# Cross-attention block: query columns put into row order at their eviction from PSUM, the residual rows loaded by one DMA, and four steps of blocks 1 to 3 moved

## The chip, the core and the metric

The kernel runs on one core of a Trainium2 chip. The core has five engines with a queue of instructions each, worked off in order: TensorE (PE, matrix products into PSUM; its weight loads are listed as PEld), VectorE (DVE), ScalarE (ACT), GpSimd (POOL) and SyncE (SP), which here issues every DMA. Engines wait for one another by semaphores. The metric is the device time of one execution in microseconds, the median of several runs. Before the change it is 1155.88 us (three runs, 1151.93 to 1157.17). Profiles come from one further execution each.

## What is computed

For 16 batches of 1024 rows of 512 numbers, with 64 context rows and one condition vector a batch, all float32:

```python
xq  = ada_ln(x_q,  t_vec, Wss_q)      # layer norm, scale and shift from t_vec
xkv = ada_ln(x_kv, t_vec, Wss_kv)
q = (xq @ Wq + bq)                    # 16 heads of 32
k, v = split(xkv @ Wkv + bkv)
attn = softmax(q @ k.T / sqrt(32))    # over the 64 context rows
out = attn @ v
return x_q + (out @ Wp + bp)          # residual rows added at the end
```

## The kernel before

**Blocks.** The rows are worked in 32 blocks of 512 rows (`NB` = 32 by batches of 16 times `BPB` = 2; the code's assertions fix `B` = 16), so block `i` is one half of batch `i // 2`. A block's x tile is `[128 partitions, t = 4, 512]`: partition p and index t hold row 128 t + p.

**Steps of a block**, each a function that issues its instructions on fixed engines:

- `load_x(i)` (L104): one 1 MB DMA. `q_stats`, `q_scale` (L248, L254): row statistics on DVE (L234, L235), a square root on ACT (L240), a reciprocal on DVE (L241) and two small operations on POOL (L242, L243). `hidden` (L269): four normalisations in place on ACT (L265).
- `turn` and `move` (L394 to L416): four 32x32 block transposes on DVE (L399) into `ht`, then 16 DMAs of 64 KB (L412) that give `xt`, features on partitions. The row 128 t + 32 g + b of the block now stands in column (g, t, b). Only block 0 is turned by TensorE instead (`first_features`) and keeps its columns in the order of rows.
- `queries(i, o)` for o = 0 to 3 (L435): eight matrix instructions `pq` (L445), then one ACT eviction with bias into `qt` (L452). The columns of `qt` stay in the order (g, t, b).
- `scores(i, z)` for the two halves z of the keys (L456): 32 small matmuls `ps` (L463) into two PSUM tiles of the pool `ps_s`, which has two buffers; for each a maximum on DVE (`m`, L474) and then a copy to SBUF on ACT (L481). The next user of `ps_s` waits for these copies.
- `maxima` (L500) combines the halves and spreads them (`mb`, L495, DVE); `subtract` (L506) takes them off the two score tiles, by default on POOL; `weights` (L512) is the exponential on ACT; `sums`, `inverse` (L516, L529) are on DVE; `divide` (L536) is on POOL by default.
- `mix(i)` (L543): 64 small matmuls `po` (L559), into `ps_s` or, with `apart=False`, into four banks of the pool `ps_m`, which has four buffers; `mixed` copies them to `ot` on ACT (L579).
- `project(i, g)` (L583): eight matrix instructions `pp` (L586) on 128 columns of `ot`, into a bank of `ps_m`; `projected` (L597) adds the residual on DVE into `ob` (L599; three buffers) and issues the 256 KB write of the result (L600). With `later=True` the caller places `projected` itself.
- `load_residual(i)` (L118): four DMAs of 256 KB (L123) bring the same rows of x again, in the order that `project` gives; `residual` adds the projection's bias to them on POOL (L276).

Since the columns of `ot` stand in the order (g, t, b), `project(i, g)` yields the rows 128 t + 32 g + b for one g: four runs of 32 rows. `by_group` (L110) is the view that both the residual load and the result's write use. For block 0 the view is 128 consecutive rows:

```python
if i == 0:
    return rows[g * P : (g + 1) * P, :]
return rows.rearrange("(t g p) h -> g t p h", t=NT, g=4)[g]
```

**What sets the order.** The program is scheduled by hand (`manual_schedule`): each engine runs its instructions in the order in which the calls stand in the text. L605 to L727 write blocks 0 to 2 out call by call, L730 to L784 are a loop over the blocks 3 to 29 (`NB - 2` = 30), and L788 to L834 write out the last two blocks, y = 30 and z = 31. In the loop the residual rows of block i are asked for after the first queries of block i + 1; near the end `load_residual(NB - 1)` stands behind `move` (L758) and `load_residual(y)` behind `project(y - 2, 3)` (L792). The tile of the residual rows of block i takes the place of that of block i - 2, so its load waits for `projected(i - 2, 3)`.

Of the kernel before, what the change touches and what calls it, by code (L numbers as in the profile page):

```python
# [9 lines left out]
F32 = mybir.dt.float32  # L10
AF = mybir.ActivationFunctionType
# [4 lines left out]
P = 128  # L16
# [4 lines left out]
def cross_attention_block(  # L21
# [36 lines left out]
    nc = tc.nc  # L58

    B, LQ, H = x.shape  # L60
# [5 lines left out]
    TB = 512  # L66
    NT = TB // P
    BPB = LQ // TB
# [7 lines left out]
    xpool = ctx.enter_context(tc.tile_pool(name="xpool", bufs=2))  # L76
# [5 lines left out]
    obpool = ctx.enter_context(tc.tile_pool(name="obpool", bufs=3))  # L82
# [7 lines left out]
    def bank(name):  # L90
        return ps_m.tile([P, TB], F32, tag="mm", name=name)
# [5 lines left out]
    ctx_tiles, x_tiles, r_tiles = {}, {}, {}  # L97

    def load_context(b):
        t = kvpool.tile([P, H], F32, tag="ctx", name=f"ctx_{b}")  # L100
        nc.sync.dma_start(t, context[b : b + 2].rearrange("b k h -> (b k) h"))
        ctx_tiles[b] = t

    def load_x(i):  # L104
        b, s = divmod(i, BPB)
        t = xpool.tile([P, NT, H], F32, tag="x", name=f"x_{i}")
        nc.sync.dma_start(t, x[b, s * TB : (s + 1) * TB, :].rearrange("(t p) h -> p t h", p=P))
        x_tiles[i] = t

    def by_group(a, i, g):  # L110

        b, s = divmod(i, BPB)
        rows = a[b, s * TB : (s + 1) * TB, :]
        if i == 0:
            return rows[g * P : (g + 1) * P, :]
        return rows.rearrange("(t g p) h -> g t p h", t=NT, g=4)[g]

    def load_residual(i):  # L118

        tag = "r" if i < NB - 1 else "x"  # L120
        r = xpool.tile([P, 4, H], F32, tag=tag, name=f"r_{i}")
        for g in range(4):
            nc.sync.dma_start(r[:, g, :], by_group(x, i, g))  # L123
        r_tiles[i] = r

    w_ss = {}
# [30 lines left out]
    b_p_sb = const.tile([P, H], F32, name="b_p_sb")  # L157
# [74 lines left out]
    def row_stats(mv, r):  # L232
        bs = small.tile([P, 6], F32, tag="bs", name="bs")
        nc.vector.bn_stats(bs, r)  # L234
        nc.vector.bn_aggr(mv, bs)  # L235
# [12 lines left out]
    def q_stats(i, ts=range(NT)):  # L248
        if ts[0] == 0:
            q_mv[i] = small.tile([P, NT, 2], F32, tag="mvq", name=f"mvq_{i}")  # L250
        for t in ts:
            row_stats(q_mv[i][:, t, :], x_tiles[i][:, t, :])

    def q_scale(i):  # L254
        q_rstd[i] = rstd_of(q_mv.pop(i), NT, "q")

    def kv_stats(b):
        kv_mv[b] = small.tile([P, 1, 2], F32, tag="mvk", name=f"mvk_{b}")
        row_stats(kv_mv[b][:, 0, :], ctx_tiles[b])
# [9 lines left out]
    def hidden(i, ts):  # L269

        for t in ts:
            normalise(x_tiles[i][:, t, :], x_tiles[i][:, t, :], q_rstd[i], t)

    def residual(i):
        for g in range(4):
            nc.gpsimd.tensor_add(r_tiles[i][:, g, :], r_tiles[i][:, g, :], b_p_sb)  # L276


    k_tiles, v_tiles, xk_tiles, hk_tiles = {}, {}, {}, {}
# [77 lines left out]
    xt_tiles, qt_tiles, wq_tiles, ht_tiles = {}, {}, {}, {}  # L357


    bqs = const.tile([P, NC, BW], F32, name="bqs")  # L360
# [45 lines left out]
    def move(i):  # L406

        ht = ht_tiles.pop(i)
        xt = qpool.tile([P, 4, NC, NT * 32], F32, tag="xt", name=f"xt_{i}")
        for k in range(4):  # L410
            for g in range(4):
                nc.sync.dma_start(  # L412
                    xt[32 * k : 32 * k + 32, g],
                    ht[32 * g : 32 * g + 32, k].rearrange("p c t b -> p c (t b)"),
                )
        xt_tiles[i] = xt  # L416
# [18 lines left out]
    def queries(i, o, spare=False):  # L435

        xt, b = xt_tiles[i], i // BPB
        if o == 0:
            qt_tiles[i] = qpool.tile([P, NC, TB], F32, tag="qt", name=f"qt_{i}")
        if spare:  # L440
            pq = ps_s.tile([P, 2, TB], F32, tag="s", name=f"pq_{i}_{o}")[:, 0, :]
        else:
            pq = bank(f"pq_{i}_{o}")
        for c in range(NC):
            nc.tensor.matmul(  # L445
                pq.rearrange("p (g n) -> p g n", g=4),
                lhsT=wq_tiles[b][:, c, o * P : (o + 1) * P],
                rhs=xt[:, :, c, :],
                start=(c == 0),
                stop=(c == NC - 1),  # L450
            )
        nc.scalar.activation(qt_tiles[i][:, o, :], pq, AF.Identity, bias=bqs[:, o, b : b + 1])  # L452

    s_tiles, m_tiles = {}, {}

    def scores(i, z):  # L456

        kt, qt = k_tiles[i // BPB], qt_tiles[i]
        pss = [ps_s.tile([P, 2, TB], F32, tag="s", name=f"ps_{i}_{z}_{e}") for e in range(2)]
        for r in range(HPC):  # L460
            rows = slice(32 * r, 32 * r + 32)
            for c in range(NC):
                nc.tensor.matmul(  # L463
                    pss[r // 2][32 * c : 32 * c + 32, r % 2, :],
                    lhsT=kt[rows, c, z * HK : (z + 1) * HK],
                    rhs=qt[rows, c, :],
                    start=True,
                    stop=True,
                )
        if z == 0:  # L470
            m_tiles[i] = small.tile([P, 2, HPC, NJ], F32, tag="m2", name=f"m2_{i}")
        s_sb = big.tile([P, HPC, TB], F32, tag="big", name=f"s_{i}_{z}")
        for e in range(2):
            nc.vector.tensor_reduce(  # L474
                m_tiles[i][:, z, 2 * e : 2 * e + 2, :],
                pss[e].rearrange("p r (j a) -> p r j a", a=32),
                AX.X,
                ALU.max,
                apply_transpose=True,
            )  # L480
            nc.scalar.copy(s_sb[:, 2 * e : 2 * e + 2, :], pss[e])  # L481
        s_tiles[i, z] = s_sb

    def both(dst, src, op):

        nc.vector.tensor_reduce(dst, src.rearrange("p z r j -> p (r j) z"), AX.X, op)
# [13 lines left out]
    def maxima(i):  # L500

        m = small.tile([P, HPC * NJ], F32, tag="m", name=f"m_{i}")
        both(m, m_tiles.pop(i), ALU.max)
        mb_tiles[i] = spread(i, m, f"mb_{i}")

    def subtract(i, eng=nc.gpsimd, zs=(0, 1)):  # L506
        for z in zs:
            eng.tensor_tensor(s_tiles[i, z], s_tiles[i, z], mb_tiles[i], ALU.subtract)  # L508
# [7 lines left out]
    def sums(i, z):  # L516
        if z == 0:
            l_tiles[i] = small.tile([P, 2, HPC, NJ], F32, tag="l2", name=f"l2_{i}")
        nc.vector.tensor_reduce(  # L519
            l_tiles[i][:, z],  # L520
            s_tiles[i, z].rearrange("p r (j a) -> p r j a", a=32),
            AX.X,
            ALU.add,
            apply_transpose=True,
        )
# [3 lines left out]
    def inverse(i):  # L529

        v = small.tile([P, HPC * NJ], F32, tag="v", name=f"v_{i}")
        both(v, l_tiles.pop(i), ALU.add)
        nc.vector.reciprocal(v, v)
        vb_tiles[i] = spread(i, v, f"vb_{i}")

    def divide(i, eng=nc.gpsimd):  # L536
        vb = vb_tiles.pop(i)
        for z in range(2):
            eng.tensor_tensor(s_tiles[i, z], s_tiles[i, z], vb, ALU.mult)  # L539

    po_tiles, ot_tiles = {}, {}
# [38 lines left out]

    pp_tiles = {}

    def project(i, g, later=False):  # L583
        pp = bank(f"pp_{i}_{g}")
        for c in range(NC):
            nc.tensor.matmul(  # L586
                pp,
                lhsT=ot_tiles[i][:, c, g * P : (g + 1) * P],
                rhs=w_p_sb[:, c, :],
                start=(c == 0),  # L590
                stop=(c == NC - 1),
            )
        pp_tiles[i, g] = pp
        if not later:
            projected(i, g)

    def projected(i, g):  # L597
        ob = obpool.tile([P, H], F32, tag="ob", name=f"ob_{i}_{g}")
        nc.vector.tensor_add(ob, pp_tiles.pop((i, g)), r_tiles[i][:, g, :])  # L599
        nc.sync.dma_start(by_group(out, i, g), ob)  # L600
        if g == 3:
            r_tiles.pop(i)


# [59 lines left out]
    divide(0)  # L664
    queries(2, 0)
    scores(1, 0)
    q_stats(3, (0, 1))
    queries(2, 1)
    scores(1, 1)
    maxima(1)  # L670
    queries(2, 2)
    q_stats(3, (2, 3))
    q_scale(3)
    subtract(1)
    mix(0, apart=False)
    mixed(0)
    queries(2, 3, spare=True)
    hidden(3, range(NT))
    turn(3, range(NT))
    move(3)  # L680
    project(0, 0)
    q_stats(4)
    kv_stats(2)
    weights(1, 0)
    sums(1, 0)
    weights(1, 1)
    project(0, 1)
    q_scale(4)
    kv_scale(2)
    context_hidden(2)  # L690
    residual(1)
    sums(1, 1)
    project(0, 2)


    load_x(5)
    scores(2, 0)
    inverse(1)
    project(0, 3)
    scores(2, 1)  # L700
    divide(1, nc.vector)
    maxima(2)
    subtract(2)
    load_residual(2)
    queries(3, 0)
    hidden(4, range(NT))
# [81 lines left out]
    y, z = NB - 2, NB - 1  # L788
# [41 lines left out]
    mix(z)  # L830
    mixed(z)
    project(y, 3)
    for g in range(4):
        project(z, g)  # L834

# [1 line left out]
_INS = [  # L837
# [37 lines left out]
```

## Time and profile before

| | |
|---|---|
| median of three runs | 1155.88 us (1151.93 to 1157.17) |
| profiled execution, its own time | 1154.13 us |
| span of the profiled instructions | 1152.3 us |
| mean granted TensorE clock | 0.994 |
| DVE busy | 789.0 us (68%) |
| ACT busy | 643.5 us (56%) |
| POOL busy | 708.3 us (61%) |
| DMA moved | 145.28 MB, mean 126 GB/s |
| L445 `pq` / L586 `pp` on PE | 467.2 / 462.7 us, 1024 matrix instructions each |
| L452 eviction of the queries on ACT | 128 of 686 ns |
| L276 residual add on POOL | 128 of 1278 ns, 84.8 us of waiting for the loads of r before them |

The page gives busy time and its share of the span for each engine; groups of instructions by source line, with their number, the busy time, the mean of one and the idle time of the engine before them with what ended it; and a chain of work, followed back from the last instruction to whatever released each step. Other views are the waits (who waited for whom), the timeline (instructions in order of time, merged, with the idle time before each in brackets) and tables of busy time by stretch. "DMA share" is the busy share of the core's 16 DMA engines. All times count from the start of the span.

### The profile page before, as it was taken

Reading aid. Unit: us, or ns where it says so; the run is one execution under the profiler, and the core shown is the slowest. Engines: PE = TensorE matmul, PEld = TensorE weight load, DVE = VectorE, ACT = ScalarE, POOL = GpSimd, SP = SyncE. Lnnn points to the kernel's source line nnn. Section 1 sums busy time; section 2 is a strip of 40 time slices with the busy share of each in tenths; the row PEclk is TensorE's granted clock in tenths of the full one; section 3 lists DMA queues with packets and bytes.
Section 4 is the critical chain, followed back from the end, with each engine's and each line's share of the span. In section 5 each row is a group of like instructions: output and inputs, shape, how many; then the busy total and the mean of one; then the engine's idle time right before and its main releaser. Section 6 shows DMA issues by size and latency. Waiting matters only on the chain.

```text
span 1152.3 us, 18883 instructions
## 1 busy us (share of the span) xinstructions
PE 1121.2 (97%) x7578; PEld 488.8 (42%) x7578; DVE 789.0 (68%) x968; ACT 643.5 (56%) x752; POOL 708.3 (61%) x332
## 2 busy tenths in 40 slices
PE   6999999999999999999999999999999999999797
PEld 3533354344544445444443445343454444544242
DVE  4679657766577775767757676766657776566592
ACT  4665736656265673657546565665636667265330
POOL 0064775776576674787656678477666677487330
PEclk9999999999999999999999999999999999999899
DMA  9534334343433343443433443333433333333212
GB/s 355 173 126 145 104 99 135 131 131 121 124 113 126 134 134 112 131 127 107 137 121 125 131 132 105 128 131 123 131 102 128 137 134 124 113 104 99 98 29 82
DMA packets 79944, 145.28 MB, mean 126 GB/s; under 512 B 9928, under 2 KB 10080, under 8 KB 79856
## 3 DMA queue, kind: packets, MB, share of 16 engines
q1 hardware_dynamic: 79856, 144.07, 38.9%
q8 instruction: 60, 0.98, 0.3%
q14 instruction: 28, 0.23, 0.1%
HBM read 77.97 MB, written 33.55 MB: 97 GB/s over the span
## 4 chain that ended last, share of the span: by engine, by line
PE 91%; DVE 4%; DMA 2%; ACT 1%; POOL 1%; issue 1%; SPq 0%; DVEq 0%; POOLq 0%
PE pq L445 37%; PE pp L586 36%; PE po L559 6%; PE ps L463 6%; PE pv L338 3%; PE pk L310 2%; DMA out_dram<-ob 1%; DVE l L519 1%; POOL s L539 1%; DMA wss_q<-in_L_xcond_Wss_q_dram 1%; DVE m L474 1%; DVE ob L599 0%; DVE mb L495 0%; DVE s L508 0%; DVE bs L234 0%
## 5 line engine op out<-in xcount | busy, mean ns | idle before, releaser
L445 PE MATMUL pq<-xt,wq 128*128 128x512 f32 x1024 | 467.2, 600 | 0.0
L586 PE MATMUL pp<-w_p_sb,ot 128*128 128x512 f32 x1024 | 462.7, 596 | 0.0
L508 POOL TENSOR_TENSOR s<-s,mb 128x2048 f32<-128x2048 f32 x58 | 262.3, 4548 | 224.6 <-DVE mb L495 224.6
L445 PEld LDWEIGHTS pq<-xt,wq 128*128 128x128 f32 x1024 | 188.8, 190 | 261.6 <-issue 259.9
L586 PEld LDWEIGHTS pp<-w_p_sb,ot 128*128 128x128 f32 x1024 | 191.2, 190 | 254.4 <-issue 244.7
L539 POOL TENSOR_TENSOR s<-s,vb 128x2048 f32<-128x2048 f32 x60 | 270.2, 4528 | 36.7 <-DVE vb L495 30.5
L481 ACT COPY s<-ps 128x1024 f32<-128x1024 f32 x128 | 129.4, 1012 | 240.2 <-DVE m L474 232.8
L276 POOL TENSOR_TENSOR r<-r,b_p_sb 128x512 f32<-128x512 f32 x128 | 161.3, 1278 | 84.9 <-DMA r<-in_x_dram 84.8
L599 DVE TENSOR_TENSOR ob<-pp,r 128x512 f32<-128x512 f32 x128 | 85.8, 672 | 163.4 <-PE pp L586 128.4
L452 ACT ACTIVATE qt<-pq,bqs 128x512 f32<-128x512 f32 x128 | 87.8, 686 | 161.2 <-PE pq L445 158.0
L519 DVE TRANSPOSE_TENSOR_REDUCE l<-s 128x64 f32<-128x2048 f32 x64 | 147.4, 2305 | 32.3 <-ACT s L514 32.1
L474 DVE TRANSPOSE_TENSOR_REDUCE m<-ps 128x32 f32<-128x1024 f32 x128 | 152.3, 1228 | 23.9 <-PE ps L463 23.7
L514 ACT ACTIVATE s<-s 128x2048 f32<-128x2048 f32 x64 | 122.2, 1911 | 30.7 <-POOL s L508 26.0
L234 DVE BATCH_NORM_STATS2 bs<-x 128x6 f32<-128x512 f32 x128 | 85.5, 668 | 41.0 <-DMA x<-in_x_dram 40.9
L265 ACT ACTIVATE x<-x,rstdq 128x512 f32<-128x512 f32 x128 | 96.6, 809 | 5.8 <-POOL rstdq L243 5.8
L399 DVE STREAM_TRANSPOSE ht<-x 128x512 f32<-128x512 f32 x124 | 78.1, 683 | 10.6 <-ACT x L265 7.2
L559 PE MATMUL po<-s,vt 32*32 32x512 f32 x2048 | 78.1, 612 | 7.4 <-ACT s L481 7.4
L463 PE MATMUL ps<-qt,kt 32*32 32x512 f32 x2048 | 75.9, 600 | 3.3 <-ACT s L481 2.4
L495 DVE STREAM_TRANSPOSE mb<-m 128x2048 f32<-128x2048 f32 x32 | 74.0, 2312 | 6.4 <-POOL s L539 3.1
L495 DVE STREAM_TRANSPOSE vb<-v 128x2048 f32<-128x2048 f32 x32 | 74.0, 2311 | 3.2
L579 ACT COPY ot<-po 128x1024 f32<-128x1024 f32 (+1 forms) x66 | 61.9, 990 | 18.8 <-PE po L559 16.0
L559 PEld LDWEIGHTS po<-s,vt 32*32 32x32 f32 x2048 | 26.6, 104 | 53.7 <-issue 48.0
(73 smaller groups left out, 447.5 us busy)
## 6 DMA issues: line engine op xcount, KB each, us to landing
x<-in_x_dram SPq DMA_DIRECT2D x32, 1024.0 KB
r<-in_x_dram SPq DMA_DIRECT2D x128, 256.0 KB
out_dram<-ob SPq DMA_DIRECT2D x128, 256.0 KB
xt<-ht SPq DMA_DIRECT2D x496, 64.0 KB
wss_q<-in_L_xcond_Wss_q_dram SPq DMA_DIRECT2D x2, 1024.0 KB
ctx<-in_ctx_dram SPq DMA_DIRECT2D x8, 256.0 KB
wss_kv<-in_L_xcond_Wss_kv_dram SPq DMA_DIRECT2D x2, 1024.0 KB
w_kv_sb<-in_L_xcond_Wkv_dram SPq DMA_DIRECT2D x1, 2048.0 KB
```

Source lines behind the costliest of these rows:

```text
L276: nc.gpsimd.tensor_add(r_tiles[i][:, g, :], r_tiles[i][:, g, :], b_p_sb)
L445: nc.tensor.matmul(pq.rearrange("p (g n) -> p g n", g=4), lhsT=wq_tiles[b][:, c, o * P : (o + 1) * P], rhs=xt[:, :, c, :], start=(c == 0), ...
L463: nc.tensor.matmul(pss[r // 2][32 * c : 32 * c + 32, r % 2, :], lhsT=kt[rows, c, z * HK : (z + 1) * HK], rhs=qt[rows, c, :], start=True, s ...
L474: nc.vector.tensor_reduce(m_tiles[i][:, z, 2 * e : 2 * e + 2, :], pss[e].rearrange("p r (j a) -> p r j a", a=32), AX.X, ALU.max, apply_tra ...
L481: nc.scalar.copy(s_sb[:, 2 * e : 2 * e + 2, :], pss[e])
L495: nc.vector.transpose(t, src.unsqueeze(2).to_broadcast([P, HPC * NJ, 32]))
L508: eng.tensor_tensor(s_tiles[i, z], s_tiles[i, z], mb_tiles[i], ALU.subtract)
L514: nc.scalar.activation(p, p, AF.Exp, scale=SCALE)
L519: nc.vector.tensor_reduce(l_tiles[i][:, z], s_tiles[i, z].rearrange("p r (j a) -> p r j a", a=32), AX.X, ALU.add, apply_transpose=True,)
L539: eng.tensor_tensor(s_tiles[i, z], s_tiles[i, z], vb, ALU.mult)
L559: nc.tensor.matmul(po[c][32 * r : 32 * r + 32, :], lhsT=vt[rows, z, 32 * r : 32 * r + 32], rhs=p[rows, r, :], start=(z == 0), stop=(z == 1),)
L586: nc.tensor.matmul(pp, lhsT=ot_tiles[i][:, c, g * P : (g + 1) * P], rhs=w_p_sb[:, c, :], start=(c == 0), stop=(c == NC - 1),)
```

## The change

Three things are altered.

1. `queries` writes `qt` in the order of rows for all blocks but 0: source and destination of the ACT eviction are viewed with the axes g, t, b, and the destination's are (t, g, b) in memory. All that follows (scores, maxima, `ot`) then has its columns in the order of rows.
2. `by_group` goes. A new `rows_of` gives the view "row 128 t + p at partition p, index t" that `load_x` had. The residual rows come by one DMA of 1 MB instead of four of 256 KB, and a project's result, now 128 consecutive rows, is written to one index t of the same view.
3. In the calls written out for blocks 1 to 3, the statistics of block 3 are taken in one piece and their scale sooner; the subtraction of block 1 is asked for right after its maxima; the hidden rows of block 3 are split in two around `mix(0)`; the statistics of block 4 go ahead of `project(0, 0)`, and the context's behind the first exponentials; three of block 0's `projected` are put later; `residual(1)` goes ahead of `q_scale(4)`; and `subtract(2)` goes from POOL to DVE.

```diff
+    def rows_of(a, i):
+        b, s = divmod(i, BPB)
+        return a[b, s * TB : (s + 1) * TB, :].rearrange("(t p) h -> p t h", p=P)
...
-        r = xpool.tile([P, 4, H], F32, tag=tag, name=f"r_{i}")
-        for g in range(4):
-            nc.sync.dma_start(r[:, g, :], by_group(x, i, g))
+        r = xpool.tile([P, NT, H], F32, tag=tag, name=f"r_{i}")
+        nc.sync.dma_start(r, rows_of(x, i))
...
-        nc.scalar.activation(qt_tiles[i][:, o, :], pq, AF.Identity, bias=bqs[:, o, b : b + 1])
+        dst = qt_tiles[i][:, o, :]
+        if i > 0:
+            dst = dst.rearrange("p (t g b) -> p g t b", t=NT, g=4)
+            pq = pq.rearrange("p (g t b) -> p g t b", g=4, t=NT)
+        nc.scalar.activation(dst, pq, AF.Identity, bias=bqs[:, o, b : b + 1])
...
-        nc.sync.dma_start(by_group(out, i, g), ob)
+        nc.sync.dma_start(rows_of(out, i)[:, t, :], ob)
...
     scores(1, 0)
-    q_stats(3, (0, 1))
+    q_stats(3)
     queries(2, 1)
+    q_scale(3)
     scores(1, 1)
     maxima(1)
+    subtract(1)
     queries(2, 2)
-    q_stats(3, (2, 3))
-    q_scale(3)
-    subtract(1)
+    hidden(3, (0, 1))
     mix(0, apart=False)
     mixed(0)
     queries(2, 3, spare=True)
-    hidden(3, range(NT))
+    hidden(3, (2, 3))
     turn(3, range(NT))
     move(3)
+    q_stats(4)
     project(0, 0)
-    q_stats(4)
-    kv_stats(2)
     weights(1, 0)
     sums(1, 0)
     weights(1, 1)
-    project(0, 1)
+    kv_stats(2)
+    project(0, 1, later=True)
+    sums(1, 1)
+    projected(0, 1)
+    residual(1)
     q_scale(4)
     kv_scale(2)
     context_hidden(2)
-    residual(1)
-    sums(1, 1)
-    project(0, 2)
+    project(0, 2, later=True)
...
     scores(2, 0)
+    projected(0, 2)
     inverse(1)
-    project(0, 3)
+    project(0, 3, later=True)
     scores(2, 1)
+    projected(0, 3)
     divide(1, nc.vector)
     maxima(2)
-    subtract(2)
+    subtract(2, nc.vector)
     load_residual(2)
```

More of the change, by code (lines that the diff above doesn't have):

```diff
@@ L102, in load_context @@
         ctx_tiles[b] = t
+    def rows_of(a, i):
+        b, s = divmod(i, BPB)
+        return a[b, s * TB : (s + 1) * TB, :].rearrange("(t p) h -> p t h", p=P)
     def load_x(i):
-        b, s = divmod(i, BPB)
         t = xpool.tile([P, NT, H], F32, tag="x", name=f"x_{i}")
-        nc.sync.dma_start(t, x[b, s * TB : (s + 1) * TB, :].rearrange("(t p) h -> p t h", p=P))
+        nc.sync.dma_start(t, rows_of(x, i))
         x_tiles[i] = t
[L110 to L116, printed above, removed]
     def load_residual(i):
         tag = "r" if i < NB - 1 else "x"
-        r = xpool.tile([P, 4, H], F32, tag=tag, name=f"r_{i}")
-        for g in range(4):
-            nc.sync.dma_start(r[:, g, :], by_group(x, i, g))
+        r = xpool.tile([P, NT, H], F32, tag=tag, name=f"r_{i}")
+        nc.sync.dma_start(r, rows_of(x, i))
         r_tiles[i] = r
@@ L274, in residual @@
     def residual(i):
-        for g in range(4):
-            nc.gpsimd.tensor_add(r_tiles[i][:, g, :], r_tiles[i][:, g, :], b_p_sb)
+        for t in range(NT):
+            nc.gpsimd.tensor_add(r_tiles[i][:, t, :], r_tiles[i][:, t, :], b_p_sb)
     k_tiles, v_tiles, xk_tiles, hk_tiles = {}, {}, {}, {}
@@ L581, in cross_attention_block, with project @@
     pp_tiles = {}
-    def project(i, g, later=False):
-        pp = bank(f"pp_{i}_{g}")
+    def project(i, t, later=False):
+        pp = bank(f"pp_{i}_{t}")
         for c in range(NC):
@@ L587, in project @@
                 pp,
-                lhsT=ot_tiles[i][:, c, g * P : (g + 1) * P],
+                lhsT=ot_tiles[i][:, c, t * P : (t + 1) * P],
                 rhs=w_p_sb[:, c, :],
@@ L592, in project, with projected @@
             )
-        pp_tiles[i, g] = pp
+        pp_tiles[i, t] = pp
         if not later:
[L595 to L599, printed above, removed]
-        nc.sync.dma_start(by_group(out, i, g), ob)
-        if g == 3:
+            projected(i, t)
+    def projected(i, t):
+        ob = obpool.tile([P, H], F32, tag="ob", name=f"ob_{i}_{t}")
+        nc.vector.tensor_add(ob, pp_tiles.pop((i, t)), r_tiles[i][:, t, :])
+        nc.sync.dma_start(rows_of(out, i)[:, t, :], ob)
+        if t == NT - 1:
             r_tiles.pop(i)
@@ L832, in cross_attention_block @@
     project(y, 3)
-    for g in range(4):
-        project(z, g)
+    for t in range(NT):
+        project(z, t)
 _INS = [
```

## The prediction

> **What bounds the kernel now.** I read the busy line of the page first, then the waits of PE, then the stretches, and last the chain over the final 120 us.
>
> ```profile
> PE 1121.2 (97%) x7578; PEld 488.8 (42%) x7578; DVE 789.0 (68%) x968; ACT 643.5 (56%) x752; POOL 708.3 (61%) x332
> ```
>
> PE is idle for 1152.3 - 1121.2 = 31 us only, so work saved elsewhere counts only if it ends one of PE's waits or shortens the two ends. Busy time by stretch (us, PE, PEld, DVE, ACT, POOL, then granted clock, DMA share, GB/s) shows where these are:
>
> ```profile
> 0.00:20.00 20.00, 8.65 (x87) 4.99 (x87) 7.94 (x23) 8.36 (x12) 1.11 (x8) 1.00 0.91 331
> ...
> 200.00:520.00 320.00, 320.00 (x2143) 137.77 (x2142) 220.45 (x273) 187.10 (x217) 220.89 (x100) 1.00 0.40 126
> ...
> 1070.00:1110.00 40.00, 32.57 (x235) 12.28 (x244) 29.40 (x22) 14.95 (x15) 16.55 (x8) 0.91 0.19 68
> 1110.00:1152.30 42.30, 34.31 (x167) 14.32 (x136) 20.08 (x18) 6.76 (x6) 0.00 (x0) 0.96 0.19 68
> ```
>
> From 145 to 1070 us PE has no gap: the chain repeats every 32.48 us (queries at 177.02, 209.50, 241.98), all matrix work. Nothing is to be had there. The first 20 us are weight loads, untouched. There remain the two late stretches, with 7.4 and 8.0 us of idle PE. The chain there:
>
> ```profile
> 1062.97 13.47 DMA out_dram<-ob
> ...
> 1076.54 0.69 DVE ob L599
> 1077.23 1.17 DVE m L474
> ...
> 1078.42 1.02 ACT s L481
> ...
> 1079.57 4.72 PE po L559 x64
> ```
>
> PE stops at 1072.07 and starts `mix(29)` 7.5 us later. It waits for ACT's copies of `scores(30, 1)`, these for the maxima on DVE, and DVE stands 10.29 us before the residual add of `project(28, 3)`: all three `ob` buffers await their writes. The first of these was ready at 1052.4, but SP issues it at 1062.97, behind the 16 moves of block 31 and four loads of r_31, and it needs 13.47 us to land. After the idle time the mix takes 4.72 us, against 2.28 in the loop, at a granted clock of 0.5.
>
> Why do writes land so slowly? Stretches where only residual loads and result writes move:
>
> ```profile
> 98.00:104.00 6.00, 5.25 (x36) 1.88 (x37) 5.86 (x7) 1.99 (x3) 1.48 (x2) 0.74 0.92 327
> ...
> 1068.00:1076.00 8.00, 4.14 (x36) 1.44 (x8) 0.00 (x0) 0.00 (x0) 4.13 (x4) 1.00 0.26 94
> ...
> 1130.00:1144.00 14.00, 14.00 (x34) 6.07 (x32) 3.46 (x5) 0.00 (x0) 0.00 (x0) 1.00 0.26 102
> 1145.00:1151.00 6.00, 0.00 (x0) 0.00 (x0) 0.04 (x1) 0.00 (x0) 0.00 (x0) 0.81 0.26 100
> ```
>
> At 98 us, with block 0's writes (128 consecutive rows) and an x load in flight, 0.92 of 16 engines move 327 GB/s. From 1068 on, with nothing but `by_group`'s four runs of 32 rows, it is 0.26 steadily: 4.2 of 16 engines, 102 GB/s.
>
> The Trainium skill, page "DMA: Bandwidth & Descriptors", section "Why a DMA increments its semaphore by 16 and not by 1", says a DMA uses the largest number of engines up to 16 that divides the slowest dimension of both sides; by it four runs get 4 engines and 128 rows 16. The rows here agree, and the sum below is the same with or without it.
>
> **The change, part by part.**
>
> *Loads and writes in order of rows.* Both become 128 partitions outermost, the form of the x load, so I take the 0.92 row: a lone 256 KB write goes from 256 KB / 102 GB/s = 2.6 us of data to 0.65-0.8, and 1 MB of r from 10.3 to 3.2. SP issues three fewer DMAs a block. In the tail: the moves of block 31 start when `ht` is ready (1046.06, unchanged) and stop waiting on r_29's slow landing; 16 x 0.63 us ends them at about 1056 instead of 1060.3. r_31 is one issue, the write of `ob` follows at about 1057 and lands, behind 1 MB of r_31, by 1063. DVE needs that buffer at 1067.4, when `pp` is done, so its wait ends with some 4 us to spare. Then add to 1068.1, maxima to 1070.5, copies to 1071.6, and PE, done with its queries at 1072.07, runs on: mix from 1072.1 to 1074.4 instead of 1084.29. **Gain 9.9 us** (7.5 idle, 2.4 of slow mix). If the write landed late after all, each us past 1067.4 costs one.
>
> What is late next? `divide(30)` on POOL must end before `mix(30)`, now wanted at 1098.5. DVE's chain from the maxima moves 8.9 us forward; inverse ends near 1086.6, r_30 (asked for near 1069, landed by 1075) has had its adds by 1080, divide runs 1086.7 to 1095.7: 2.8 us spare. `mix(31)` needs DVE's divide, ending at 1114.5 against PE at 1114.8: spare, but little.
>
> *The last write.* `ob` ends at 1145.04, the span at 1152.3: 7.3 us of DMA and closing. Data time falls by 1.9 us, and slow first packets are spread over more engines. Ends 1.5 and 3.5; I take **2.5**, since the data time alone gives 1.9.
>
> *Residual as one load.* POOL's first add must now await all of r instead of a quarter, but at 3.2 us for the whole against 2.6 for a quarter it lands about when the first quarter does now. The 84.8 us of POOL waiting is cover, not path: worth nothing, and costs nothing.
>
> *Permuted eviction.* 124 evictions of 686 ns write runs of 32 numbers. No ACT row shows that. Nearest: DVE's block transpose writes such runs in 683 ns for 512 columns, against 2312/4 = 578 in runs of full length, and a plain add takes 672. So 0 to +105 ns, no gain possible as the count is the same; I take the nearer row, about 0. Even 105 x 124 = 13 us lies in ACT's 509 idle us; exposed is one place, `scores(31, 0)` straight behind the last eviction: 0.1 us.
>
> *Blocks 1 to 3.* Two row statistics more (0.85 each) and the reciprocal, which waits for ACT's square root, come ahead of the maxima of `scores(1, 1)`: these start at 73.3 instead of 71.64. So copies and the eviction of `queries(2, 2)` end 1.4 late (77.3), and `mix(0)`, whose fourth bank waited just for that eviction at 75.94, stands 1.4 us. Against it, POOL subtracts block 1 from 78.4 instead of 80.69, since the scale no longer precedes it; the exponentials end about 1.2 us sooner. Up to `scores(2, 1)` the two cancel: by the queue on DVE (statistics 86.1-89.4, add, sums, statistics, sums, add, reciprocals, maxima from 96.5 against 96.38) it starts near 99.2 (98.71) and ends near 100.8 (100.86). Next, `subtract(2)` on DVE costs 2 x 2.28 = 4.6 us there, ahead of turn, statistics and sums; DVE had 5.74 us of idle time before those sums. It puts the maxima of `scores(3, 0)` at 133.1 against 132.59, so PE resumes 0.5 us later than its 134.92.
>
> The clock has a say in it:
>
> ```profile
> 97.44:100.85 3.41, 2.10 (x32) 0.37 (x32) 3.27 (x5) 2.02 (x2) 2.04 (x2) 1.00 0.92 308
> 100.85:104.26 3.41, 3.41 (x12) 1.51 (x5) 3.41 (x4) 0.58 (x1) 0.00 (x0) 0.50 0.82 311
> 131.57:134.98 3.41, 2.94 (x15) 1.01 (x17) 3.41 (x5) 1.01 (x1) 3.40 (x1) 1.00 0.31 18
> ```
>
> A stretch with PE busy 2.10 of 3.41 us was followed by one at half clock, 1.7 us lost; 2.94 was not. If PE waits less at 99 us it keeps its clock, arrives early at `scores(3, 1)`, waits longer there and may lose it then. Below +0.5 it can't go, since DVE's queue sets that. So +0.5 to +2.2; I take **+1.0**, nearer the first, since one slow stretch was paid before too.
>
> A rule that speaks against the move: the skill's page "SBUF — State Buffer", section "Who interferes with whom", says a DVE instruction with two SBUF inputs and a GpSimd one that reads SBUF exclude each other. `subtract(2)` on DVE would meet `residual(2)` on POOL (r_2 lands near 111); by it up to three adds of 1.27 us, 3.8 us more, hence +4.8. Before, no such pair overlaps, so no row here shows it.
>
> **Sum.** 9.9 + 2.5 - 1.0 = 11.4 us. Against the profiled execution's own 1154.13 that is 1142.7; the median shown is 1.75 higher, which would give 1144.5. I forecast 1143.5.
>
> **Rivals.**
> - *Blocks 2 and 3 are dear*: DVE is late at `scores(3, 1)` by several us, as it is 68% busy and gets 4.6 us of POOL's work; if half or all of those 4.6 are exposed besides the 2.2 above, the loss is 4.5 to 6.8 instead of 1: 1147 to 1149.3. For: maxima waiting at 132.59 had no spare. Against: 5.74 us of idle before it.
> - *The tail's wait is replaced*: `divide(30)` or `divide(31)` ends late and returns 3 to 6 us: 1146 to 1149. For: 2.8 us spare and less.
> - *The change does not do what it says*: writes still move at 100 GB/s; nothing in the tail, 1 us lost: 1155 to 1157. Against: the x load's rows at 327.
> - *Slower*: the permuted eviction at L452. A loop block has 187.10/320 x 32.48 = 19.0 us of ACT, 16.2 without its four evictions. From 4.06 us an eviction ACT binds the 27 loop blocks; from 4.2 on it eats the gain and 5.8 us more, at 4.5 it costs 27 x 1.8 = 48 us: 1191. Against: 683 beside 672 ns.
>
> **How the numbers follow.** Forecast 0.62, dear blocks 0.17, replaced wait 0.09, no effect 0.08, slower 0.04. 0.5% (5.8 us) is about what a measurement can tell from no change; faster by more means under 1150.1: 0.62 and most of the second and third, 0.84; same 0.12; slower 0.04. Range: low end 1154.13 - (9.9 + 3.5) - 2.2 (the lowest run lies so far under the profile) = 1138.5, rounded down to 1138; high end the dear blocks and the replaced wait, 1149, and 1 us of scatter: 1150. That leaves out the last two cases.
>
> **What would show it.** Right: residual adds and `ob` without waits for DMA, no DMA row in the chain near 1063, po at 2.3 us in `mix(29)`, DMA share near 0.9 in bursts, some 5 us from the last `ob` to the end. The permuted eviction is right at 680-790 ns. Wrong: a PE gap over 2 us before `scores(3, 1)`, DVE's `s` at L508 over 2.3 us, or a share of 0.26 that stays.

## The result

The changed kernel takes 1143.9 us (median of four runs, 1142.84 to 1144.34), the kernel before 1154.24 in the same comparison (1151.93 to 1157.17): a ratio of 0.9908, 95% interval 0.988 to 0.9935. It is faster by 0.9%, some 10 us. The profiled execution has a span of 1142.4 us against 1152.3.

PE does the same work and is idle for 21.5 us in place of 31.1. The page of the changed kernel, its busy line and its loads and writes (number, size, median us from issue to landing):

```profile
PE 1120.9 (98%) x7578; PEld 488.7 (43%) x7578; DVE 793.3 (69%) x970; ACT 643.7 (56%) x752; POOL 705.5 (62%) x330
...
r<-in_x_dram SPq DMA_DIRECT2D x32, 1024.0 KB, 6.7
out_dram<-ob SPq DMA_DIRECT2D x128, 256.0 KB, 2.2
```

The chain of the last 120 us of the changed kernel, which answers to the one that held a DMA of 13.47 us:

```profile
1071.71 1.07 PE ps L461 x32
1072.78 3.63 PE pq L439 x8
1076.41 2.28 PE po L557 x62
1078.69 10.50 PE pq L439 x24
...
1138.75 0.69 DVE ob L597
```

No DMA stands in it, `mix(29)` follows the queries without a gap, and its matrix work takes 2.28 us instead of 4.72. Of the DMA waits of DVE's residual add (35.1 us before) none is left.

Setting the two timelines beside each other at fixed events tells where the 9.96 us of span went. "Shift" is the time of the event after, less that before.

| stretch | event at its end | before | after | shift gained in it |
|---|---|---|---|---|
| start | first half of the scores of block 0 done, `scores(0, 1)` | 47.30 | 48.72 | +1.4 |
| blocks 0 to 3 | `mix(3)` | 180.59 | 184.86 | +2.9 |
| loop | `mix(28)` | 1039.59 | 1043.87 | 0.0 |
| tail | `mix(30)` | 1108.39 | 1102.80 | -9.9 |
| end | last matrix instruction to end of span | 8.03 | 3.66 | -4.4 |

The start holds weight loads that the change doesn't touch, and the first queries begin between 20.2 and 22.6 us over all profiles of this study, so +1.4 is taken as scatter.

The end was long before because writes queued. Nine writes ran back to back on the four engines from 1126.1 to 1151.4 us, one landing every 2.57 us, and DVE's adds waited for their buffers:

```profile
1138.71 0.69 DVE L599 TENSOR_TENSOR ob<-pp,r 128x512 f32<-128x512 f32 x1 [1.87 <-DMA out_dram<-ob]
1141.28 0.69 DVE L599 TENSOR_TENSOR ob<-pp,r 128x512 f32<-128x512 f32 x1 [1.88 <-DMA out_dram<-ob]
```

The last write was issued at 1145.07 and landed at 1151.41, 6.3 us later; for 3.8 of these the engines still moved the writes in front of it. After the change each of the last five writes is through its data in 0.8 us, before the next is issued, and the last lands 2.0 us after its issue.

Of the +2.9 of blocks 0 to 3, PE's timeline before has these lines at `scores(3, 1)`:

```profile
134.92 2.22 PE L463 MATMUL ps<-qt,kt 32*32 32x512 f32 x32 [0.47 <-ACT s L481]
137.07 3.70 PE L445 MATMUL pq<-xt,wq 128*128 128x512 f32 x8
```

and that of the changed kernel, with a stop in `mix(0)` too:

```profile
78.54 2.15 PE L557 MATMUL po<-s,vt 32*32 32x512 f32 x40 [0.87 <-ACT qt L450]
...
136.12 3.09 PE L461 MATMUL ps<-qt,kt 32*32 32x512 f32 x32 [2.60 <-ACT s L479]
139.15 5.91 PE L439 MATMUL pq<-xt,wq 128*128 128x512 f32 x8
```

PE stops 0.87 us in `mix(0)`, and at `scores(3, 1)` it waits 2.60 us where it waited 0.47. Behind that wait eight instructions take 5.91 us that take 3.70 at full clock. The table by stretch of the changed kernel (us, then busy time of PE, PEld, DVE, ACT, POOL, granted clock, DMA share, GB/s) has the clock of that stretch, and the DMA rate in the tail:

```profile
136.79:143.61 6.82, 6.82 (x30) 2.11 (x23) 4.58 (x4) 2.44 (x3) 5.39 (x4) 0.50 0.87 318
1060.00:1070.00 10.00, 10.00 (x54) 4.10 (x53) 5.41 (x5) 1.27 (x2) 7.58 (x2) 1.00 0.69 197
```

Where the share lay at 0.26 whenever residual rows and results were alone, r_31, the first writes behind it and the end of the moves now fill 0.69 of 16 engines and are done by 1070.

### The profile page after: what moved, and what is told of

Read it like the earlier page. It is cut to its first block, busy times and chain, and to the rows that moved or that the text cites. A ratio compares the mean times of both kernels' runs of the same rounds, so it can differ in the third digit from the quotient of the medians.

```text
span 1142.4 us, 18791 instructions
## 1 busy us (share of the span) xinstructions
PE 1120.9 (98%) x7578; PEld 488.7 (43%) x7578; DVE 793.3 (69%) x970; ACT 643.7 (56%) x752; POOL 705.5 (62%) x330
## 4 chain that ended last, share of the span: by engine, by line
PE 94%; DVE 3%; DMA 1%; ACT 1%; issue 1%; SPq 0%; POOL 0%; DVEq 0%; ACTq 0%
PE pq L439 39%; PE pp L584 37%; PE po L557 6%; PE ps L461 6%; PE pv L332 3%; PE pk L304 3%; DMA wss_q<-in_L_xcond_Wss_q_dram 1%; DVE l L517 1%; DVE bs L228 1%; DVE m L472 1%; DVE ht L393 0%; PE pss_q L197 0%; DVE ob L597 0%; DVE s L506 0%; PE pkt L284 0%
## 5 line engine op out<-in xcount | busy, mean ns | idle before, releaser
L506 POOL TENSOR_TENSOR s<-s,mb 128x2048 f32<-128x2048 f32 x56 | 253.3, 4548 | 215.4 <-DVE mb L493 213.4
L270 POOL TENSOR_TENSOR r<-r,b_p_sb 128x512 f32<-128x512 f32 x128 | 167.2, 1347 | 38.6 <-DMA r<-in_x_dram 38.6
```

Of the source, the lines that this page charges most:

```text
L270: nc.gpsimd.tensor_add(r_tiles[i][:, t, :], r_tiles[i][:, t, :], b_p_sb)
```

## The experiments

Theory A before them: the tail and the end come from the form of the DMAs, and the +2.9 from the new order of calls in blocks 1 to 3. Rivals: that the number of DMAs matters and not their form; that the faster DMAs themselves disturb blocks 1 to 3. All times are medians, ratios are against the kernel before of the same comparison.

### 1. The rows without the new order

```diff
-    q_stats(3)
+    q_stats(3, (0, 1))
...
-    subtract(2, nc.vector)
+    subtract(2)
```

(All calls between `divide(0)` and `load_residual(2)` as before the change.)

> The change without its third part: permuted eviction, one residual load and row-order writes as in the changed kernel, the calls for blocks 1 to 3 in the order of before. Theory A (loads and writes on 16 engines give 9.9 us in the tail and 4.3 behind the last add; the new order of blocks 1 to 3 costs 2.9, nearly all of it through a longer wait before scores(3, 1) and the half clock after it): 1154.2 - 14.2 = 1140.0 us, scores(3, 1) as before, with a wait of about 0.5 us. Theory B (blocks 1 to 3 lose because the faster DMAs' bursts disturb them, the order is neutral): 1143.9, with the wait of 2.6 us still there.

Measured: 1144.58 us, 0.9909 (0.9891 to 0.9927). Neither theory is right as it stands: the time is B's, but the wait of 2.6 us before `scores(3, 1)` is gone (0.46), as A has it. The loss sits elsewhere. PE's timeline of this version:

```profile
80.21 1.54 PE L557 MATMUL po<-s,vt 32*32 32x512 f32 x32 [1.40 <-POOL s L537]
```

`mix(0)` now stands for POOL's `divide(0)`, half clock follows (3.4 us at 80.86, and 6.8 at 104.75 instead of 3.4), and from the first queries to `mix(3)` it takes 164.4 us against 160.4 before the change. POOL is late because of `residual(0)`. The loads of r and POOL's adds, in the kernel before:

```profile
58.23 2.03 SPq L123 DMA_DIRECT2D r<-in_x_dram  x4
...
61.30 4.95 POOL L276 TENSOR_TENSOR r<-r,b_p_sb 128x512 f32<-128x512 f32 x4 [19.44 <-DMA r<-in_x_dram]
```

and in the changed kernel:

```profile
59.38 0.58 SPq L117 DMA_DIRECT2D r<-in_x_dram  x1
...
65.15 4.96 POOL L270 TENSOR_TENSOR r<-r,b_p_sb 128x512 f32<-128x512 f32 x4 [22.21 <-DMA r<-in_x_dram]
```

From the issue of r_0 to the first add it is 3.1 us with four loads (of 128 consecutive rows each for block 0, before the change too) and 5.8 with one. This I had not seen; it gives a theory C, that the one load of r_0 is a cost of its own, tested in experiments 8 and 9.

### 2. The new order alone

The calls from `divide(0)` to `load_residual(2)` as in the changed kernel, all else as before.

> Only the third part of the change: the new order of calls for blocks 1 to 3 with the residual loads, writes and evictions of before. Theory A: 1154.2 + 2.9 = 1157.1 us, tail unchanged (PE idle 7.4 us before mix(29)), a wait of over 2 us before scores(3, 1) and half clock after it; up to 1159 if the four slow quarters of r_2 meet subtract(2) for longer. Theory B: 1154.2.

Measured: 1158.82 us, 1.0034 (1.002 to 1.0049): slower, so the order does cost, some 4 us. Its timeline has the long wait before `scores(3, 1)`:

```profile
112.40 5.69 DVE L508 TENSOR_TENSOR s<-s,mb 128x2048 f32<-128x2048 f32 x2
...
135.40 2.28 PE L463 MATMUL ps<-qt,kt 32*32 32x512 f32 x32 [2.27 <-ACT s L481]
```

In the profiled execution, 2 us faster than the median of the twelve runs, only 0.9 us are lost up to `mix(3)`, and half clock lasted 3.4 us there, not 6.8. Another 1.9 us are lost within the loop, without a gap of PE, and the tail gains 1.3. So the order's cost is shown by the medians; this one profile doesn't show where all of it lies.

### 3. subtract(2) back on POOL

```diff
-    subtract(2, nc.vector)
+    subtract(2)
```

> The changed kernel with subtract(2) back on POOL, nothing else. If DVE's subtraction (6.0 us there, with the waits for POOL) is what makes scores(3, 1) late: sums(2, 0) then wait for POOL's subtraction and start near 122.1 instead of 124.3, scores(3, 1) starts near 133.9 instead of 136.1 with PE waiting 0.5 us, no half clock: 1143.9 - 5.2 = 1138.7 us. If the lateness comes from the moves before it (statistics, residual adds put later): 1143.9.

Measured: 1138.65 us, 0.9863 (0.9842 to 0.9884), as expected to the tenth. PE and POOL in its timeline:

```profile
112.80 9.05 POOL L506 TENSOR_TENSOR s<-s,mb 128x2048 f32<-128x2048 f32 x2 [14.96 <-DVE mb L493]
...
133.95 2.22 PE L461 MATMUL ps<-qt,kt 32*32 32x512 f32 x32 [0.46 <-ACT s L479]
136.11 3.70 PE L439 MATMUL pq<-xt,wq 128*128 128x512 f32 x8
```

POOL needs 9.05 us for what DVE did in 6.02, and yet PE gets its scores 2.2 us sooner and keeps its clock. The engine that was 62% busy had the time; DVE's queue had not. This one word is worth 5.2 us (1143.9 less 1138.65), half as much as the 10 us that the whole change brought.

### 4. No adds beside the subtraction

```diff
-    residual(2)
     sums(2, 1)
     inverse(2)
     divide(2)
+    residual(2)
```

> The changed kernel with residual(2) called behind divide(2), so that POOL adds nothing while DVE subtracts block 2. If the two engines exclude each other there (POOL's adds took 3.32 us in place of 1.28, DVE's two subtractions 6.02 in place of 4.57): subtract(2) takes 4.57, the four adds 5.0, scores(3, 1) starts 1.5 us sooner; 1142.4 us if the half clock stays, 1139.3 if the shorter wait keeps the clock. If the long instructions have another cause (the load of r_2 landing, for instance): no change, 1143.9.

Measured: 1142.68 us, 0.9897 (0.9878 to 0.9915); the six runs (1140.81 to 1145.38) can't be told from 1143.9. The mechanism is there. In the changed kernel the two engines worked side by side:

```profile
112.10 9.09 POOL L270 TENSOR_TENSOR r<-r,b_p_sb 128x512 f32<-128x512 f32 x4 [14.22 <-DMA r<-in_x_dram]
...
112.80 6.02 DVE L506 TENSOR_TENSOR s<-s,mb 128x2048 f32<-128x2048 f32 x2
```

Here, with POOL idle beside it, DVE subtracts in 4.49 us, and the adds take 4.99 where they took 9.09:

```profile
116.49 4.49 DVE L506 TENSOR_TENSOR s<-s,mb 128x2048 f32<-128x2048 f32 x2
138.30 2.23 PE L461 MATMUL ps<-qt,kt 32*32 32x512 f32 x32 [1.08 <-ACT s L479]
143.93 4.99 POOL L270 TENSOR_TENSOR r<-r,b_p_sb 128x512 f32<-128x512 f32 x4
...
151.90 3.70 PE L584 MATMUL pp<-w_p_sb,ot 128*128 128x512 f32 x8 [1.84 <-ACT ot L577]
```

The wait before `scores(3, 1)` fell from 2.60 to 1.08, and no half clock follows it. But the adds now hold up the scale of block 5 behind them on POOL, ACT's hidden rows wait for that, its copies of `ot` too, and PE stops 1.84 us at 151.90. How much of the gain this gave back in the median isn't shown: the profiled execution is the slowest of the six, with 6.8 us at half clock from 79.74 on, beside stops of 0.87 and 0.71 us in `mix(0)`.

The same meeting stands in the tail of the changed kernel, where it costs nothing: from 1078.06 on `subtract(30)` takes 5.58 us beside the adds of r_30 (8.79), and `divide(30)` still ends 2.3 us before `mix(30)` needs it.

### 5. A fourth `ob` buffer for the kernel before

```diff
-    obpool = ctx.enter_context(tc.tile_pool(name="obpool", bufs=3))
+    obpool = ctx.enter_context(tc.tile_pool(name="obpool", bufs=4))
```

> The kernel before with a fourth buffer for the sums ob that await their write, all DMAs as before. If the stall in front of mix(29) is DVE waiting for an ob buffer, as the chain says: the wait of 10.29 us and PE's 7.4 us go, and the half clock after it, while writes still move at 102 GB/s and the last one takes as long: 1154.8 - 9.9 = 1145 us. If the late maxima come from something else that moves with the DMAs: 1154.8.

Measured: 1154.24 us, 0.9976 (0.9958 to 0.9993), a quarter of the gain. PE and POOL in the tail of this version:

```profile
1074.90 2.35 PE L559 MATMUL po<-s,vt 32*32 32x512 f32 x64
...
1088.28 1.28 POOL L276 TENSOR_TENSOR r<-r,b_p_sb 128x512 f32<-128x512 f32 x1 [11.69 <-DMA r<-in_x_dram]
...
1097.13 11.03 POOL L539 TENSOR_TENSOR s<-s,vb 128x2048 f32<-128x2048 f32 x2
...
1108.21 2.02 PE L559 MATMUL po<-s,vt 32*32 32x512 f32 x32 [5.36 <-POOL s L539]
```

The stall before `mix(29)` is gone, without any faster DMA: it was the wait for a buffer, as the chain said. But `mix(30)` then waits 5.36 us, since r_30, at 102 GB/s, keeps POOL's adds waiting and these keep `divide(30)`. The old wait had covered a second one of the same cause. Of the versions here only those with the faster loads are free of both.

### 6 and 7. The old form for the writes, and for the loads

On the version of experiment 3, with `runs_of` being the `by_group` of before for blocks after 0:

```diff
-        nc.sync.dma_start(rows_of(out, i)[:, t, :], ob)
+        nc.sync.dma_start(runs_of(out, i, t), ob)
```

> The version with subtract(2) on POOL (1138.65 us), its results written through the view of four runs of 32 rows that the kernel before used; every result row is so written to another place of its block, residual loads untouched. Theory A (the form of the DMA sets 4 or 16 engines): writes at a share of 0.26 and 102 GB/s again, last add to end 7.3 us instead of 3.0, no stall before mix(29), since r_31 is still fast and the write of the first buffer lands some 2 us in time: 1142.5 to 1143. Rival (what counts is that three DMA issues a block are saved, not the form): no change, 1138.65.

Measured: 1142.78 us, 0.9882 (0.9857 to 0.9907). In its table by stretch, the writes before and behind the last add:

```profile
1115.00:1133.00 18.00, 17.99 (x68) 7.52 (x40) 3.46 (x5) 1.93 (x2) 0.00 (x0) 1.00 0.26 94
1134.00:1140.00 6.00, 0.00 (x0) 0.00 (x0) 0.00 (x0) 0.00 (x0) 0.00 (x0) 0.68 0.24 95
```

The form alone brings back the share of 0.26 and the 8.0 us from the last matrix instruction to the end. PE has no gap in the tail. Then the loads:

```diff
-        nc.sync.dma_start(r, rows_of(x, i))
+        if i == 0:
+            nc.sync.dma_start(r, rows_of(x, i))
+        else:
+            for g in range(4):
+                nc.sync.dma_start(r[:, g, :], runs_of(x, i, g))
```

> The version with subtract(2) on POOL (1138.65 us), its residual rows loaded, for all blocks but 0, by four DMAs through the view of four runs of 32 rows; the residual rows added are so other rows of the block, writes untouched. Theory A: r_31 needs some 10 us on 4 engines and the moves before it wait for r_29, so the write of the first ob buffer is issued some 4 us later and lands some 10 us later: DVE waits about 5 us, PE the most of that, then half clock: 1144 to 1147, last write as short as before. If the writes' own form made the stall: 1138.65.

Measured: 1145.1 us, 0.9897 (0.9868 to 0.9926), inside what A gave; one of the four runs took 1141.44. The timeline of its tail:

```profile
1059.48 12.45 SPq L606 DMA_DIRECT2D out_dram<-ob  x4
...
1070.88 0.69 DVE L605 TENSOR_TENSOR ob<-pp,r 128x512 f32<-128x512 f32 x1 [4.25 <-DMA out_dram<-ob]
...
1073.91 4.12 PE L565 MATMUL po<-s,vt 32*32 32x512 f32 x64 [1.39 <-ACT s L487]
```

Writes in the new form wait behind residual rows in the old one: the first, issued at 1059.48, landed 11.3 us later. Not all of A's steps are there. The 16 moves took 10.3 us, as in the changed kernel (10.0; 14.3 before), so r_29's slow landing alone didn't hold them up, and PE waited only 1.39 us and lost more at half clock. From `mix(28)` to `mix(30)` it takes 64.5 us, against 58.9 in the changed kernel and in experiment 6, and 68.8 before. So the end belongs to the writes. Of the tail's 9.9 us the old loads alone bring back 5.6, the old writes alone nothing, and the other 4.3 show only where both have the old form.

### 8 and 9. Four loads of 128 consecutive rows

```diff
-        nc.sync.dma_start(r, rows_of(x, i))
+        for t in range(NT):
+            nc.sync.dma_start(r[:, t, :], rows_of(x, i)[:, t, :])
```

On the version of experiment 3:

> The version with subtract(2) on POOL (1138.65 us), its residual rows loaded by four DMAs of 128 consecutive rows each in place of one. Theory A (form, not number): tail as with one load. Besides, residual(0) no longer waits for the whole 1 MB (it started at 65.15 us in the changed kernel, 61.30 before) and starts some 3 us sooner, divide(0) too, and PE's second stop in mix(0), 0.95 us for POOL, goes: 1137.7. Rival (number of issues): the stall before mix(29) comes back, 1145 or more.

Measured: 1138.96 us, 0.9852 (0.9827 to 0.9878). The stall of the tail stays away with four loads: no gap there, only `scores(31, 1)` takes 0.6 us longer (1.64 for 1.07). In the profile the first add stands 3.0 us behind the issue of r_0 and the wait for POOL in `mix(0)` is gone, but in the time that is within the scatter. On the version of experiment 1:

> Rows in order and evictions permuted as in the changed kernel, blocks 1 to 3 in the order of before (1144.6 us), but the residual rows by four DMAs of 128 consecutive rows. Theory C (that version lost its early part because residual(0) on POOL awaits all of r_0, and with it divide(0), mix(0) and the half clocks after them; nothing of it is the order): residual(0) starts some 3 us after the issue instead of 5.8, no wait for POOL in mix(0), the half clock of 3.4 us after it and that of 6.8 us at 105 shrink to the one of 3.4 us of before: 1144.6 - 4.0 = 1140.6 us. Rival D (the lower number of issues or the bursts of other transfers made it lose): 1144.6.

Measured: 1142.41 us, 0.9883 (0.9868 to 0.9898). Its timeline has `residual(0)` at 3.4 us from the issue, and `mix(0)` as before the change:

```profile
59.54 2.04 SPq L118 DMA_DIRECT2D r<-in_x_dram  x4
...
62.93 4.97 POOL L271 TENSOR_TENSOR r<-r,b_p_sb 128x512 f32<-128x512 f32 x4 [19.65 <-DMA r<-in_x_dram]
...
76.29 2.99 PE L558 MATMUL po<-s,vt 32*32 32x512 f32 x64
```

From the first queries to `mix(3)` it takes 160.2 us, so the whole 4.0 us that experiment 1 lost there are back, and the profiled span is 1139.9 us. The median gained 2.2, not 4.0 (3.0 by the ratios). Theory C holds for the mechanism. Two of the three other runs took 1.5 and 2.0 us more than the profiled one, at a granted clock of 0.997 instead of 0.999; where they lost it is open.

### 10 and 11. Towards the best version

On the version of experiment 8:

```diff
-    q_stats(3)
+    q_stats(3, (0, 1))
     queries(2, 1)
-    q_scale(3)
     scores(1, 1)
+    q_stats(3, (2, 3))
     maxima(1)
-    subtract(1)
     queries(2, 2)
-    hidden(3, (0, 1))
+    q_scale(3)
+    subtract(1)
     mix(0, apart=False)
     mixed(0)
+    hidden(3, (0, 1))
     queries(2, 3, spare=True)
```

> Four residual loads and subtract(2) on POOL (1138.96 us), and the statistics of block 3 split again: the second half before maxima(1), the scale behind queries(2, 2), the hidden rows behind mixed(0). If the statistics ahead of scores(1, 1) make the eviction of queries(2, 2) late and with it mix(0): the stop of 0.87 us there falls to 0 to 0.3 us, and if the wait before scores(2, 1) doesn't take it back, 1138.1 us; if it does, 1138.96.

Measured: 1138.29 us, 0.9844 (0.9829 to 0.9858). The stop of 0.87 us in `mix(0)` is gone from its timeline; the time can't be told from 1138.96. Then `context_hidden(2)` behind `divide(1, nc.vector)`:

> As the version with the statistics split, and context_hidden(2) called behind divide(1), so that ACT copies the scores of block 2 before it waits for the context's scale on POOL: the copies start up to 0.9 us sooner, scores(2, 1) waits that much less: 1137.3 us. If DVE's maxima set that point: as the version with the statistics split.

Measured: 1138.08 us, 0.9844 (0.9831 to 0.9858); the wait before `scores(2, 1)` went from 0.35 us to nothing. It has the lowest median here, 5.8 us under the changed kernel, and all but 0.6 us of that is `subtract(2)` on POOL.

## Why the prediction was right, and where not

1143.5 us were forecast, 1143.9 measured. That it came so near is luck: two terms were wrong by 1.9 us each in opposite directions, and 1143.5 was a choice between 1142.7 and 1144.5. Two of the prediction's own signs of being wrong appeared as well: a gap over 2 us before `scores(3, 1)` (2.60) and subtractions over 2.3 us on DVE (2.73 and 3.36). The large term, the tail, was right.

- **Tail, 9.9 us forecast, 9.9 measured.** The step held in each part but one: writes on more engines, `ob` free in time, no idle time, no half clock. The moves ended when forecast (1056.0 on the clock of before), but experiment 7 doesn't bear out the reason given, r_29's slow landing. Experiment 5 shows that the wait was the buffer's, 7 that the form of the loads makes 5.6 us of the loss by itself, 6 that the form of the writes makes none without that of the loads, 8 that the number of loads doesn't. By the Trainium skill's page "DMA: Bandwidth & Descriptors", section "Why a DMA increments its semaphore by 16 and not by 1", a DMA uses the largest number of engines up to 16 that divides the slowest dimension of both sides. This trace agrees: 0.26 of 16 with four runs outermost, in experiment 6 again.
- **What is late next.** `divide(30)` was to end 2.8 us before `mix(30)` wanted it; it ended at 1100.5, 2.3 before 1102.8. The rival that the wait is replaced did not happen, but experiment 5 shows it was real: with slow loads it takes 5.4 us.
- **Last write, 2.5 forecast (1.5 to 3.5), 4.4 measured.** Mis-sized: the term counted the last write's own data time, 1.9 us, and something for slow first packets. By the trace the last write landed 6.3 us after its issue before, and 2.0 after. What the term left out is the queue: 3.8 of the 6.3 us belonged to the writes in front, while the last write's own packets took 84 ns each, none of them slow.
- **Residual as one load, "worth nothing, and costs nothing".** The step that failed. It was read off the loop, where POOL's wait is cover. In block 0 `residual(0)` stands before `divide(0)` and `mix(0)` with nothing to spare, and the first add waits 2.7 us longer. With the order of before that costs 4.0 us of the profile (experiments 1 and 9). In the new order it doesn't show in the time: with `subtract(2)` on POOL, one load and four differ by 0.3 us (1138.65 and 1138.96), which is scatter.
- **Permuted eviction, about 0.** Right: 687 ns against 686, so the rival that ended slower had no ground.
- **Blocks 1 to 3, +1.0 forecast (0.5 to 2.2), +2.9 measured.** The clock's part went as written: PE kept its clock at 101 us, came early to `scores(3, 1)`, waited longer and lost it there. PE resumed there even 0.2 us sooner than before, counted from `scores(0, 1)`, where 0.5 later was forecast as the least. What was too small is the price of the clock, 1.7 us: half clock lasted 6.8 us, not 3.4, and cost 3.1 us on PE (3.09 + 5.91 against 2.22 + 3.70 in experiment 3). The rule that the prediction left out of its sum is seen as well. By the Trainium skill's page "SBUF — State Buffer", section "Who interferes with whom", a DVE instruction with two SBUF inputs and a GpSimd one that reads SBUF exclude each other. This trace agrees: two of POOL's adds took 3.32 us against 1.28, DVE's two subtractions 2.73 and 3.36 against 2.29, 1.5 us more in sum, and in experiment 4, apart, both were short. The rival of dear blocks 2 and 3 was thus right on its cause, DVE's queue, and wrong on its size, 4.5 us or more.

## What to carry to other kernels

Look at the share of DMA engines in a stretch where only one kind of transfer moves: 0.26 of 16 pointed here to a form that could be mended, and putting the data into order where an engine writes them anyway was free. When the last write lands late, ask what stands in the queue before it. When a wait is taken away, ask which wait of the same cause it covered, and read a cost off the block where the step has least to spare, not off the loop. Work moved to the faster engine can be late there: 9.05 us on POOL beat 6.02 us on DVE by 5 us.

## What the runs showed of the hardware that was not expected

- The length of PE's wait alone doesn't tell what half clock follows. After 2.60 us it was 6.8 us, after 2.27 (experiment 2) and 1.94 us (before) 3.4, after 1.79 (experiment 1) again 6.8, after 1.40 (experiment 1, in `mix(0)`) 3.4, and after 1.84 and 1.08 us in experiment 4 none.
- A 256 KB write lands in 2.2 us (median) with 128 rows outermost. With four runs outermost, one that had the engines to itself (issued at 1101.09 in the kernel before) took 5.7 us, though the data time differs by 1.9 us only: early packets took up to 0.86 us each, the later ones 0.084.
- The runs of the kernel before spread over 1151.8 to 1158.4 us (17 runs), those of the version of experiment 11, whose profile has no half clock in the work, over 1137.8 to 1138.3 (4 runs). The fastest of the 17 had a granted clock of 0.996, the slowest 0.991. That half clock makes the spread is likely, but was not tried by itself.
